# Constants and first row loads on POOL's queue, a longer filling product in short diagonals, image totals by transposes and a DVE sum

## The chip, the cores and the metric

The kernel runs on one core of a Trainium2 chip. The metric is the device time of one execution, in microseconds (us). A core has five engines, each with its own queue of instructions that it takes in order: PE (TensorE, matrix products and transposes into the PSUM memory), DVE (VectorE), ACT (ScalarE), POOL (GpSimd) and SP (SyncE, which here only issues DMA transfers). A DMA can be issued by SP, ACT or POOL; the data is then moved by sixteen DMA engines. PE's clock is granted by a throttle, and the profile shows the granted share of full speed (1.00, or 0.50 in stretches where it was halved). PSUM has eight banks, each of 128 partitions by 512 float32 elements.

## The reference

The input x has 16 images of 64 x 64 cells with 128 features. Three parts follow each other, each added to what it is given:

```python
x = x + lstm_2d(group_norm(x), ...)           # 32 groups of 4 features, statistics per image
t = x.reshape(16, 4096, 128)
t = t + attention(layer_norm(t), ...)         # 8 heads of 16, 64 landmarks
t = t + recurrent_ffn(layer_norm(t), ...)     # batch statistics, then yt = sigmoid(wx_t + yt @ V.T)
```

The two-dimensional LSTM computes a cell from its upper and its left neighbour: five gates, each a product of the normalised x by W and of the states by U, then `c = f0*c_u + f1*c_l + i*cp`, `h = o*tanh(c)`. The attention is the Nystrom form: with q and k averaged over 64 rows at a time into 64 landmarks per head,

```python
attn1 = softmax(q @ k_l.T); attn2 = softmax(q_l @ k_l.T); attn3 = softmax(q_l @ k.T)
out = attn1 @ pinv(attn2) @ (attn3 @ v) + conv33(v)      # pinv: six iterations
return (xn + (out @ w_out + b_out))
```

The softmax of `attn3` runs over all 4096 rows of an image, so its sums and `attn3 @ v` are gathered over the whole image before they can be used.

## The kernel before, in words

**Statistics of the images** (`group_stats`, 0 to 105 us). For each of the 16 images four loads of 512 KB, issued by SP (line 115), fill tiles `gs_xb` (twelve buffers). PE transposes each in blocks (line 118) into PSUM, DVE takes `bn_stats` of 512 columns (line 119), eight times an image, and one aggregate (line 120). Lines 121 and 122 call one function of the list `aside` behind an image, the first behind the fourth image (`b - 3`). The list is `jobs[:1] + loads + jobs[1:]`: `conv_bands` (eight small products that turn the convolution's weights into bands, and ACT's copy), four functions that load the rows of the first seven LSTM units (14 DMAs on ACT's queue), and `turn_weights` (a transpose of `ffn_w` and three ACT copies). Behind the images the late constants are loaded (SP), and PE, ACT, POOL and DVE make mean and inverse deviation (`centre`, `spread`), with products on the weights as filling between.

**Constants.** Ahead of it 17 DMAs on ACT's queue bring constants: four columns (`column`), three of `conv_lines` (`cb_line` from the weights, `cb_flat` in DRAM from `cb_line`, `cb_tm` from `cb_flat`, each waiting for the one before), and ten of `attention_tiles` (eight for `at_wo`, `at_bo`, `at_wf`). POOL fills tiles by memset and builds `head_mask` by two selections; DVE's `lm_side` (line 478) reads the mask, and stands in DVE's queue among the first statistics.

**LSTM** (`lstm_grid`, 105 to 1430 us). The cells of a diagonal are computed together, diagonal after diagonal, 190 slots; a diagonal has 16 columns of data per cell, from 16 up to 1024 and back, the middle ones cut into two halves. A slot issues the gates' products with U (line 288) on top of those with W that were begun earlier (line 283), the cell's arithmetic on DVE, POOL and ACT, and the later steps of the diagonals before. Where the diagonal is not cut and has at most 144 columns, `fill(384)` adds at the slot's end a product of 384 columns into the PSUM tile `ls_hq` whose result nobody reads (line 30 in `idle_products`).

**Attention** (1640 to 3470 us). After a first image's `first_step` and a mixed `second_step`, `step(s)` handles at once several groups of 512 rows in different stages: `new` (projections; largest scores of `attn3`, `greatest`, line 1028, and DVE's maxima, line 1032), `mid` (the group eight behind: `weigh`, exponentials line 1073, POOL's sum of weights line 1100, product with V), and `first`, `cur`, `third` to `sixth` (the groups some sixteen behind: `compare` line 1135, `topmost` line 1143, the softmax of `attn1`, output, normalisation, FFN input; `measure_feed` is DVE's statistics of the FFN input, line 1252). Eight groups make an image. Where an image starts (`q == 0`, 14 times in `step`) two more things are done: the image whose largest scores are complete gets its shifts (`shift` on POOL ends in `split`, lines 1040 to 1046; `turn_split` transposes it into bank 3, line 1011, ACT copies it), and the image whose weights are complete is gathered (`gather`): `im.sums`, the product of weights and values, is transposed into bank 2, and the sum over 512 weights per row, kept as four blocks of 128 partial sums `im.total`, is taken by four products by ones, line 1118 (eight instructions in the trace), also into bank 2; DVE takes the reciprocal (line 1121) and multiplies (`at_av`, line 1124); `spread_values` (line 1020) multiplies by the pseudo-inverse. `last_step` does the same at two starts, when only the late stages are left. `greatest` needs banks 0 to 3, `weigh` banks 4 and 5 and a pair of others, `turn_top` (line 1159) bank 2.

**Recurrence** (3470 to 3637 us): the FFN's scan, whose outputs POOL adds to the result by 64 DMAs (line 1600).

**Order.** In all these stages the instructions of an engine stand in the order of the program (`manual_schedule`); the constants and memsets ahead of them are placed by a planner that moves ready instructions ahead of waiting ones. A DMA issue is an instruction of its queue: while it waits for its source or for a semaphore, nothing behind it on that queue runs. The landing of a DMA is reported on a semaphore, which the program takes in turn from a fixed set.

Of the kernel before, what the change touches and what calls it, by code (L numbers as in the profile page):

```python
# [9 lines left out]
ALU = mybir.AluOpType  # L10
AX = mybir.AxisListType
# [3 lines left out]
P = 128  # L15
# [5 lines left out]
AHEAD = 7  # L21
# [34 lines left out]
def group_stats(nc, tc, x, ident, mhalf, gmean, grstd, aside, late, filler):  # L56
# [8 lines left out]
    with ExitStack() as ctx:  # L65
# [42 lines left out]
        for b in range(B):  # L108
            v = first if b < last.b0 else last
            rows = x[b].rearrange("i j f -> (i j) f").rearrange("(p k) f -> p k f", k=K)  # L110
            st = sp.tile([P, K // 4, 6], F32, tag="st", name="gs_st")
            for q in range(K // 4):
                if q % 2 == 0:
                    xb = ld.tile([P, 8, F], F32, tag="xb", name="gs_xb")
                    nc.sync.dma_start(out=xb, in_=rows[:, 4 * q : 4 * q + 8, :])
                tp = ps.tile([P, 4, P], F32, tag="tp", name="gs_tp")
                for k in range(4):
                    nc.tensor.transpose(tp[:, k, :], xb[:, q % 2 * 4 + k, :], ident)
                nc.vector.bn_stats(st[:, q, :], tp.rearrange("p k n -> p (k n)"))
            nc.vector.bn_aggr(v.mv[:, b - v.b0, :], st.rearrange("p q s -> p (q s)"))  # L120
            if 0 <= b - 3 < len(aside):
                aside[b - 3]()
            if b == last.b0:
                centre(first, nc.scalar.copy, nc.gpsimd)
# [53 lines left out]
def lstm_grid(nc, tc, x, fixed, stats, ident, mhalf, gmean, grstd, t1, acc, filler):  # L178
# [18 lines left out]
    with ExitStack() as ctx:  # L197
# [193 lines left out]
        def slot(t):  # L391
# [34 lines left out]
            if v and v.ns == S and v.cols <= NARROW:  # L426
                fill(384)

        with tc.manual_schedule(
# [4 lines left out]
        ):  # L434
            stats([lambda a=a: [load(v, nc.scalar) for v in units[a : min(a + 2, AHEAD)]] for a in range(0, AHEAD, 2)])
            wk = ctx.enter_context(tc.tile_pool(name="ls_wk", bufs=2, reuse_waits="tile"))
# [16 lines left out]
def column(nc, pool, vec, name):  # L453
    a = pool.tile([P, 1], F32, name=name)
    nc.scalar.dma_start(out=a, in_=vec.rearrange("(p o) -> p o", o=1))
    return a
# [283 lines left out]
def conv_lines(nc, pool, conv_w, dram):  # L740

    H, _, KS, _ = conv_w.shape
    T = 32
    W = T + KS - 1
    flat = dram.tile([H, T + W], F32, name="cb_flat")
    line = pool.tile([H, T + W], F32, name="cb_line")
    nc.vector.memset(line, 0.0)
    nc.scalar.dma_start(out=line[:, T - 1 : T - 1 + KS], in_=conv_w.rearrange("h a k c -> h (a k c)"))
    nc.scalar.dma_start(out=flat, in_=line)
    tm = pool.tile([T, H, W], F32, name="cb_tm")  # L750
    nc.scalar.dma_start(out=tm, in_=bass.AP(tensor=flat.tensor, offset=flat.offset, ap=[[1, T], [T + W, H], [1, W]]))
# [18 lines left out]
def attention_tiles(nc, cp, sp, ps, dram, late, shape, values, conv_w, w_out, b_out, ffn_w, ident):  # L770
# [6 lines left out]
    C = 4  # L777
# [6 lines left out]
    for h in range(H):  # L784
        r = PLACE[h] * W2 + h % 2 * DH
        nc.scalar.dma_start(out=wo[r : r + DH], in_=w_out[h * DH : (h + 1) * DH])
    B = values.shape[0]
# [6 lines left out]
    bo = cp.tile([P, F], F32, name="at_bo")  # L794
    nc.scalar.dma_start(out=bo, in_=b_out.rearrange("(o f) -> o f", o=1).to_broadcast([P, F]))
    wf = cp.tile([P, P], F32, name="at_wf")
    nc.scalar.dma_start(out=wf, in_=ffn_w)
    wfT = cp.tile([P, P], F32, name="at_wfT")
# [47 lines left out]
def attention(nc, tc, t1, gamma, beta, wqkv, ident, mhalf, fixed, xp, rows, qm, km, pinvT, vd, t2, wx, wx_stats, out, ahead):  # L846
# [20 lines left out]
    with ExitStack() as ctx:  # L867
# [140 lines left out]

        def turn_split(im):
            r = bank(3, [P, P])  # L1010
            nc.tensor.transpose(r, split.rearrange("p n s -> p (n s)"), ident)
# [101 lines left out]
        def gather(im):  # L1113

            at = bank(2, [P, C, P])
            nc.tensor.transpose(at[:, 0, :], im.sums, ident)
            for n in range(NP):
                nc.tensor.matmul(at[:, 1, W2 * n : W2 * n + 2], im.total[:, n, :], ones[:, 0:2], start=True, stop=True)
            im.AV = sm.tile([P, NP, DH], F32, tag="av", name="at_av")
            rs = sm.tile([P, NP], F32, tag="rs", name="at_rs")  # L1120
            nc.vector.reciprocal(rs, at[:, 1, :].rearrange("p (n c) -> p n c", n=NP)[:, :, 0])
            for j in range(2):
# [277 lines left out]
        def step(s):  # L1400
# [334 lines left out]
def kernel(ctx: ExitStack, tc: tile.TileContext, ins: dict, out: bass.AP):  # L1735
# [43 lines left out]
    with tc.tile_pool(name="at_c", bufs=1) as ac, tc.tile_pool(name="at_x", bufs=1) as xp, tc.tile_pool(  # L1779
# [4 lines left out]
        with tc.tile_pool(name="first", bufs=1) as first:  # L1784
# [5 lines left out]
            with tc.tile_pool(name="ls_c", bufs=1) as lc:  # L1790
# [46 lines left out]
```

## Time and profile before

| | us |
|---|---|
| three runs | 3631.91, 3635.04, 3635.63 |
| median | 3635.04 |
| the profiled execution's own time | 3638.43 |
| its span | 3636.9 |

The table of stretches, asked for by stage (busy us of each engine; granted clock, GB/s):

| stage | us | PE | DVE | ACT | POOL | clock | GB/s |
|---|---|---|---|---|---|---|---|
| statistics | 0 to 105 | 80.95 | 87.79 | 3.85 | 20.37 | 0.93 | 335 |
| LSTM | 105 to 1430 | 1296.63 | 1163.88 | 826.92 | 1031.65 | 0.99 | 78 |
| landmarks, pseudo-inverse | 1430 to 1640 | 195.08 | 104.40 | 91.13 | 69.64 | 1.00 | 32 |
| attention | 1640 to 3190 | 1535.03 | 1309.44 | 1236.38 | 1171.54 | 1.00 | 161 |
| last steps | 3190 to 3470 | 250.53 | 219.65 | 208.79 | 142.58 | 0.99 | 183 |
| recurrence | 3470 to 3637 | 141.68 | 97.61 | 132.78 | 53.47 | 0.95 | 223 |

How to read a profile's line: a group of instructions is given as line of the kernel, engine, operation, tile written <- tiles read, partitions x elements, count, then busy time and the mean duration of one in ns, then the idle time ahead of them and what ended it. In a timeline, the first number is the start in us from the span's start, the second the duration. In a list of waits, `SPq L115 <- DMA ls_xt<-in_x_dram: 3.9, 2, 2.8` says that SP's queue, at line 115, waited for the landing of that transfer 3.9 us in all, twice, at most 2.8. "PEld" is the load of weights into PE, which runs beside its products.

### The profile page before, as it was taken

The numbers are of one execution on the slowest core, as the hardware profiler recorded it, in microseconds if no ns is written. First come the engines' busy times: TensorE is split into PE (matmuls) and PEld (weight loads), VectorE is DVE, ScalarE is ACT, GpSimd is POOL, SyncE is SP. The second block draws the span as 40 slices with busy tenths as digits, with TensorE's granted clock in tenths as the row PEclk, the third lists the DMA queues.
The fourth block names the chain that finished last, engine by engine and source line by source line (L and its number), as shares of the span: only waits on it lengthen the run. The fifth ranks groups of instructions, "written<-read, shape, count | busy, mean of one in ns | idle before, by whom it ended". The sixth has DMA issues, their size and how long they took to land. (4 is left out here: it accounts for less than half of the span.)

```text
span 3636.9 us, 106193 instructions
## 1 busy us (share of the span) xinstructions
PE 3499.9 (96%) x40438; PEld 2343.7 (64%) x40438; DVE 2982.8 (82%) x7005; ACT 2499.9 (69%) x5126; POOL 2489.2 (68%) x3843
## 2 busy tenths in 40 slices
PE   7899999999999998999999999999999999997988
PEld 5666665545567666985666666666666666654777
DVE  8699999998889887544888888888888888888665
ACT  0466556656667665445788888888888888876787
POOL 1577877777788885434777777777777777785223
PEclk9999999999999999999999999999999999999999
DMA  9223232333333321023677777777777777667799
GB/s 339 83 76 80 80 86 80 84 84 83 85 88 86 81 76 38 4 63 92 147 185 187 164 162 163 166 167 163 164 166 166 165 164 168 157 143 187 201 273 182
DMA packets 834210, 484.50 MB, mean 133 GB/s; under 512 B 304672, under 2 KB 800672, under 8 KB 833696
## 3 DMA queue, kind: packets, MB, share of 16 engines
q1 hardware_dynamic: 814026, 442.55, 47.8%
q0 software_dynamic: 17728, 34.61, 5.3%
q8 instruction: 322, 5.28, 0.6%
q14 instruction: 192, 1.57, 0.1%
q10 hardware_dynamic: 1942, 0.50, 0.1%
HBM read 239.21 MB, written 238.29 MB: 131 GB/s over the span
## 5 line engine op out<-in xcount | busy, mean ns | idle before, releaser
L1100 POOL TENSOR_TENSOR at_total<-at_total,at_e 128x512 f32<-128x512 f32 x472 | 603.1, 1278 | 228.3 <-ACT at_e L1073 208.6
L290 ACT ACTIVATE ls_g<-ls_z,ls_b 128x304 f32<-128x304 f32 (+26 forms) x950 | 494.0, 545 | 225.0 <-PE ls_z L288 192.7
L283 PE MATMUL ls_z<-ls_xn,ls_w 128*128 128x432 f32 (+28 forms) x1700 | 586.1, 492 | 1.5 <-POOL ls_xn L275 1.2
L283 PEld LDWEIGHTS ls_z<-ls_xn,ls_w 128*128 128x128 f32 x1700 | 309.6, 191 | 189.4 <-issue 98.1
L288 PE MATMUL ls_z<-ls_hsum,ls_u 128*128 128x304 f32 (+26 forms) x1140 | 369.7, 461 | 0.0
L1032 DVE TENSOR_REDUCE at_mxq<-at_bank 128x1 f32<-128x512 f32 x512 | 314.9, 677 | 53.0 <-PE at_bank L1028 53.0
L323 POOL TENSOR_TENSOR ls_tt<-ls_ve,mhalf 128x8 f32<-128x8 f32 (+2 forms) x190 | 312.7, 1646 | 19.8 <-DVE ls_ve L322 4.2
L288 PEld LDWEIGHTS ls_z<-ls_hsum,ls_u 128*128 128x128 f32 x1140 | 211.6, 194 | 128.6 <-issue 78.4
L1177 ACT ACTIVATE at_eT<-at_bank 128x512 f32<-128x512 f32 x512 | 264.5, 604 | 42.1 <-PE at_bank L1172 41.5
L406 ACT ACTIVATE ls_g<-ls_cell 128x304 f32<-128x304 f32 (+26 forms) x190 | 93.2, 491 | 268.1 <-DVE ls_cell L405 267.8
L288 PE MATMUL ls_z<-ls_h,ls_u 128*128 128x304 f32 (+26 forms) x760 | 256.2, 460 | 12.3 <-DVE ls_h L410 12.3
L402 POOL TENSOR_TENSOR ls_g<-ls_g,ls_cell 128x304 f32<-128x304 f32 (+26 forms) x190 | 180.1, 948 | 127.7 <-ACT ls_g L290 113.0
L340 ACT ACTIVATE ls_tt<-ls_tt,ls_nb 128x128 f32<-128x128 f32 (+9 forms) x632 | 261.0, 478 | 5.6 <-POOL ls_tt L323 5.0
L979 PE MATMUL at_bank<-at_xT,wqkv 128*32 128x512 f32 (+1 forms) x1684 | 262.8, 602 | 2.0 <-DVE at_cmx L1143 1.1
L275 POOL TENSOR_TENSOR ls_xn<-ls_xn,grstd 128x272 f32<-128x272 f32 (+40 forms) x186 | 209.9, 1129 | 76.2 <-DVE ls_xn L270 71.2
L1143 DVE TENSOR_REDUCE at_cmx<-at_bank 128x8 f32<-128x512 f32 x256 | 175.6, 686 | 103.8 <-PE at_pair L1135 102.1
L1248 ACT COPY at_fx<-at_bank 128x512 f32<-128x512 f32 x128 | 133.7, 1044 | 142.9 <-PE at_bank L1244 138.3
L1619 DVE SCALAR_TENSOR_TENSOR rc_y<-rc_w,rc_scale,rc_z 128x256 f32<-128x256 f32 x344 | 154.6, 481 | 86.3 <-PE rc_z L1606 84.5
L1238 ACT ACTIVATE at_z<-at_u,at_nb,at_r 128x128 f32<-128x128 f32 x512 | 209.6, 484 | 4.6 <-POOL at_nb L1233 4.5
L288 PEld LDWEIGHTS ls_z<-ls_h,ls_u 128*128 128x128 f32 x760 | 141.9, 193 | 107.8 <-issue 53.2
L1600 POOL DMA_DIRECT2D out_dram<-rc_tt x64 | 77.4, 1209 | 168.4 <-ACT rc_tt L1597 145.0
L1193 DVE STREAM_TRANSPOSE at_t<-at_bank 128x512 f32<-128x512 f32 x256 | 167.9, 695 | 25.3 <-PE at_bank L1184 25.2
(281 smaller groups left out, 9683.8 us busy)
## 6 DMA issues: line engine op xcount, KB each, us to landing
at_win<-vd SPq DMA_DIRECT2D x256, 256.0 KB
t<-ls_tt SPq DMA_DIRECT2D x392, 130.0 KB
at_T<-t SPq DMA_DIRECT2D x128, 264.0 KB
gs_xb<-in_x_dram SPq DMA_DIRECT2D x64, 512.0 KB
at_xh<-t SPq DMA_DIRECT2D x128, 256.0 KB
vd<-at_v SPq DMA_DIRECT2D x128, 256.0 KB
t<-at_u SPq DMA_DIRECT2D x128, 256.0 KB
out_dram<-at_u SPq DMA_DIRECT2D x128, 256.0 KB
```

Of the source, the lines that this page charges most:

```text
L275: eng.tensor_tensor(a, a, norm(v, grstd), ALU.mult)
L283: nc.tensor.matmul(v.z[g][:, : v.total], wt[g], v.xn[:, : v.total], start=True, stop=True)
L288: nc.tensor.matmul(view(v, v.first.z[g]), ut[g], hin, start=False, stop=True, skip_group_check=True)
L290: nc.scalar.activation(a[:, : v.cols], z, AF.Tanh if g == 4 else AF.Sigmoid, bias=bt[g])
L323: nc.gpsimd.tensor_tensor(v.tt[:, 0:k, F + 2 : F + 4], ve[:, :, :k].rearrange("p r k -> p k r"), mhalf[:, : 2 * k].rearrange("p (k r) -> p ...
L340: nc.scalar.activation(v.tt[:q, k, F + 4 :], v.tt[:q, k, 0:F], AF.Identity, bias=v.nb[:q, k : k + 1], scale=v.tt[:q, k, F + 3 : F + 4],)
L402: nc.gpsimd.tensor_mul(v.a[1], v.a[1], v.cl)
L979: nc.tensor.matmul(out[r], lhsT[:, r], rhs, start=True, stop=True)
L1032: nc.vector.tensor_reduce(gr.im.mxq[:, n : n + 1, gr.g], gr.s[n], AX.X, ALU.max)
L1100: eng.tensor_tensor(total, total, e[:, :, c, :], ALU.add)
L1177: nc.scalar.activation(gr.eT[:, n], gr.s[n], AF.Exp)
L1238: nc.scalar.activation(gr.z[:, c, :], gr.u[:, c, :], AF.Identity, bias=gr.nb[:, c : c + 1], scale=gr.r3[:, c : c + 1])
```

## The change

Three edits.

1. The 17 constants and the 14 row loads of the first LSTM units are issued by POOL's queue (`nc.gpsimd`) instead of ACT's. In `group_stats` the list `aside` starts behind the seventh image instead of the fourth, and it holds the loads first, then `conv_bands` and `turn_weights`.
2. In diagonals of at most 64 columns (`4 * B`) the filling product of 384 columns is followed by one of 256.
3. `gather` transposes the four blocks of `im.total` into bank 2, DVE sums the 512 columns and takes the reciprocal; the transpose of `im.sums` goes to bank 3. In `step`, `gather` comes earlier, right behind `topmost`, at the place where `measure_feed` stands in the other steps (which then comes behind `measure(fourth, (2, 3))`), and `turn_split` uses bank 2 instead of 3.

```diff
-            if 0 <= b - 3 < len(aside):
-                aside[b - 3]()
+            if 0 <= b - 6 < len(aside):
+                aside[b - 6]()
...
-                fill(384)
+                fill(384, *[256] * (v.cols <= 4 * B))
...
-            stats([lambda a=a: [load(v, nc.scalar) for v in units[a : min(a + 2, AHEAD)]] for a in range(0, AHEAD, 2)])
+            stats([lambda a=a: [load(v, nc.gpsimd) for v in units[a : min(a + 2, AHEAD)]] for a in range(0, AHEAD, 2)])
...
-    nc.scalar.dma_start(out=a, in_=vec.rearrange("(p o) -> p o", o=1))
+    nc.gpsimd.dma_start(out=a, in_=vec.rearrange("(p o) -> p o", o=1))
...
-        nc.scalar.dma_start(out=wo[r : r + DH], in_=w_out[h * DH : (h + 1) * DH])
+        nc.gpsimd.dma_start(out=wo[r : r + DH], in_=w_out[h * DH : (h + 1) * DH])
...
-        def turn_split(im):
-            r = bank(3, [P, P])
+        def turn_split(im, k=3):
+            r = bank(k, [P, P])
...
-            at = bank(2, [P, C, P])
+            total, at = bank(2, [P, NP, P]), bank(3, [P, 1, P])
+            for n in range(NP):
+                nc.tensor.transpose(total[:, n, :], im.total[:, n, :], ident)
             nc.tensor.transpose(at[:, 0, :], im.sums, ident)
-            for n in range(NP):
-                nc.tensor.matmul(at[:, 1, W2 * n : W2 * n + 2], im.total[:, n, :], ones[:, 0:2], start=True, stop=True)
...
-            nc.vector.reciprocal(rs, at[:, 1, :].rearrange("p (n c) -> p n c", n=NP)[:, :, 0])
+            nc.vector.tensor_reduce(rs, total, AX.X, ALU.add)
+            nc.vector.reciprocal(rs, rs)
...
-            if sixth:
+            if start and was:
+                gather(was.im)
+            elif sixth:
                 measure_feed(sixth)
...
-            if start and was:
-                gather(was.im)
...
-                turn_split(mid.im)
+                turn_split(mid.im, 2 if was else 3)
...
+            if start and was and sixth:
+                measure_feed(sixth)
...
-                        group_stats(nc, tc, x, ident, mhalf, gmean, grstd, jobs[:1] + loads + jobs[1:], late, wqkv)
+                        group_stats(nc, tc, x, ident, mhalf, gmean, grstd, loads + jobs, late, wqkv)
```

The other constants (`cb_line`, `cb_flat`, `cb_tm`, `at_bo`, `at_wf`) are edited in the same way as `at_wo`.

More of the change, by code (lines that the diff above doesn't have):

```diff
@@ L747, in conv_lines @@
     nc.vector.memset(line, 0.0)
-    nc.scalar.dma_start(out=line[:, T - 1 : T - 1 + KS], in_=conv_w.rearrange("h a k c -> h (a k c)"))
-    nc.scalar.dma_start(out=flat, in_=line)
+    nc.gpsimd.dma_start(out=line[:, T - 1 : T - 1 + KS], in_=conv_w.rearrange("h a k c -> h (a k c)"))
+    nc.gpsimd.dma_start(out=flat, in_=line)
     tm = pool.tile([T, H, W], F32, name="cb_tm")
-    nc.scalar.dma_start(out=tm, in_=bass.AP(tensor=flat.tensor, offset=flat.offset, ap=[[1, T], [T + W, H], [1, W]]))
+    nc.gpsimd.dma_start(out=tm, in_=bass.AP(tensor=flat.tensor, offset=flat.offset, ap=[[1, T], [T + W, H], [1, W]]))
     turn = pool.tile([T, T], F32, name="cb_turn")
@@ L794, in attention_tiles @@
     bo = cp.tile([P, F], F32, name="at_bo")
-    nc.scalar.dma_start(out=bo, in_=b_out.rearrange("(o f) -> o f", o=1).to_broadcast([P, F]))
+    nc.gpsimd.dma_start(out=bo, in_=b_out.rearrange("(o f) -> o f", o=1).to_broadcast([P, F]))
     wf = cp.tile([P, P], F32, name="at_wf")
-    nc.scalar.dma_start(out=wf, in_=ffn_w)
+    nc.gpsimd.dma_start(out=wf, in_=ffn_w)
     wfT = cp.tile([P, P], F32, name="at_wfT")
```

## The prediction

> **What bounds the kernel now.** I read the page of the profile first. PE is busy 96% of the span, but a share over stages with different limits says little, so I went by stretches: the first 105 us (statistics of the sixteen images), the diagonals up to 1430 us, and the attention steps from 1640 to 3190 us.
>
> ```profile
> PE 3499.9 (96%) x40438; PEld 2343.7 (64%) x40438; DVE 2982.8 (82%) x7005; ACT 2499.9 (69%) x5126; POOL 2489.2 (68%) x3843
> ```
>
> Second, the table by stretches of 10 us (stretch, length, busy PE, PEld, DVE, ACT, POOL, granted clock, DMA share, GB/s).
>
> ```profile
> 10.00:20.00 10.00, 4.89 (x30) 4.03 (x28) 4.82 (x10) 1.28 (x1) 8.61 (x15) 0.92 0.76 260
> 20.00:30.00 10.00, 8.59 (x61) 7.09 (x60) 9.51 (x18) 0.00 (x0) 7.98 (x19) 0.91 1.01 398
> 40.00:50.00 10.00, 5.65 (x32) 4.50 (x32) 6.18 (x11) 0.00 (x0) 0.00 (x0) 0.78 0.79 233
> 50.00:60.00 10.00, 6.95 (x46) 6.45 (x47) 6.39 (x11) 0.00 (x0) 0.00 (x0) 0.71 0.98 370
> 80.00:90.00 10.00, 9.17 (x64) 6.43 (x62) 9.93 (x19) 0.00 (x0) 0.00 (x0) 1.00 1.02 419
> ```
>
> Undisturbed, DMA brings 419 GB/s and DVE is full (9.93 of 10). From 10 to 20 and from 40 to 60 us both drop. Third, the waits of SP's queue say why:
>
> ```profile
> SPq L115 <- DMA ls_xt<-in_x_dram: 3.9, 2, 2.8
> SPq L115 <- DMA cb_tm<-cb_flat: 3.8, 1, 3.8
> SPq L115 <- DMA cb_flat<-cb_line: 2.6, 1, 2.6
> SPq L115 <- DMA at_wo<-in_L_attn_w_out_dram: 1.2, 2, 0.8
> ```
>
> A load of x (line 115) has no use for these constants and rows, and yet waits for them. The trace gives each issue the semaphore of its landing: SP's and ACT's issues take turns on the same eight (100, 102 to 108), so a new issue waits for the landing eight issues back, whoever issued it; POOL's 68 issues use eight others (111 to 118). While ACT issues 17 constants (1.0 to 13.4 us) and 14 row loads (34.1 to 44.8 us), few of the eight places hold a 512 KB load of x.
>
> Fourth, the timeline of one step that starts an image (line 1135 at 1932.72 us):
>
> ```profile
> 1936.53 0.95 PE L1118 MATMUL at_bank<-at_ones,at_total 128*128 128x2 f32 x8
> ...
> 1937.18 0.22 POOL L1046 TENSOR_SCALAR at_split<-at_mx 128x4 f32<-128x4 f32 x1
> ...
> 1937.46 0.33 PE L1011 MATMUL at_bank<-ident,at_split 128*128 128x128 f32 x1
> ...
> 1937.74 0.46 DVE L1124 TENSOR_TENSOR at_av<-at_bank,at_rs 64x64 f32<-64x64 f32 x2
> ...
> 1938.85 0.62 PE L1028 MATMUL at_bank<-at_KT,qm 32*128 32x512 f32 x2
> ...
> 1942.72 0.38 PE L1159 MATMUL at_bank<-at_identb,at_top 128*128 128x128 bf16 x4 [0.47 <-ACT at_g L1022]
> ```
>
> An ordinary step takes 12.69 us (1920.04 to 1932.72) with PE without a gap; this one 15.80. Fifth, the filling product in a short diagonal, while the clock is 0.5 and late at full clock:
>
> ```profile
> 116.72 1.65 PE L30 MATMUL ls_hq<-wqkv,ident 128*128 128x384 f32 x2
> ```
>
> ```profile
> 1414.61 0.91 PE L30 MATMUL ls_hq<-wqkv,ident 128*128 128x384 f32 x2 [0.88 <-DVE ls_tt L301]
> ```
>
> **The sum's base.** The profiled execution took 3638.43 us (span 3636.9); the median of the runs shown is 3635.04, 3.4 us lower. I add up against 3638.43 and take 3.4 off at the end.
>
> **Part 1: constants and first row loads on POOL.** DVE paces the statistics: in the undisturbed images the aggregates (line 120) are 5.14 us apart (68.49, 73.63, 78.76). Sixteen make 82.2 us. The first statistic starts at 6.80 and the last aggregate ends at 104.82, so 15.8 us are stalls: the gaps between aggregates exceed 5.14 by 3.1 and 4.2 us in the first two images (constants) and by 2.9 and 5.5 us in the sixth and seventh (row loads). With POOL issuing, all eight places hold loads of x, 10 us of transfer at 1.25 us each.
>
> What stays: the first six statistics run 0.85 us apart at the cold clock instead of 0.64, 1.4 us in all; DVE's wait of 1.4 us for `lm_side`, which needs POOL's second selection of `head_mask` at 13.02; and what small packets take from x, for which no row exists: 0.48 MB at 419 GB/s is 1.2 us, and I take 1.5. POOL itself: its 31 new issues have no row here. The bounds are ACT's own issues (0.30 to 0.77 us) and POOL's output DMAs (64 at 1.209 us, line 1600); I take 1.209, the same engine: 37 us of a queue that idles 70.0 us before line 95, so later work is covered. Early it is not: POOL stands 8.65 us before its first selection, `cb_flat` waits for `cb_line` (2.93 to 7.88 us before) and `cb_tm` for `cb_flat` (7.94 to 12.04), now with POOL's queue behind them. If two or three issues slip in front of the second selection, `lm_side` comes 2.5 to 3.5 us later. I take 2.9. Sum: 15.8 - 1.4 - 1.4 - 1.5 - 2.9 = 8.6 us gained, bounds 13.0 (no slip, no loss to packets) and a loss (rival 1). Late issues, `load` of SP and the centring chain keep their places behind the last aggregate. Moving `conv_bands` and `turn_weights` behind the 11th and 12th image (before: the fourth and ninth) shifts 0.91 and 0.27 us of PE that DVE's pace hides; without that cover they would cost just these.
>
> The Trainium skill says otherwise. "DMA: Bandwidth & Descriptors", section "Issuing engines are not separate DMA queues", holds that DMAs from scalar, sync and gpsimd end on the same 16 engines and that spreading them saves only issue time. By the waits above, what is shared here is the eight places and not the engines, whose share falls to 0.76. By that page of the Trainium skill this part would bring 0; this trace shows the waits and cannot show the rest.
>
> **Part 2: filling products.** A 256-wide product is added where a diagonal has at most 64 columns: four at the beginning, four at the end. The 384-wide one holds PE for 0.75 us at full clock (1414.61 until the next gate product at 1415.36), so 256 cost 0.50, cold 1.0. The first diagonal hides it in a gap of 0.39 us; in the others the fill stands on the chain, since it waits for `ls_tt` and the next gates queue behind it: 0.1 + 7 x 0.50 = 3.6 us. Gain: the clock was 0.5 from 113.9 to 127.6 us. Gate to gate the diagonals there took 4.51 and 4.58 us, at full clock a like one 3.07 (1412.29 to 1415.36): 2.9 us; the third is cold for 4.8 us, at the same ratio 1.5; at the end (cold 1417.8 to 1428.0) 0.46 and 0.8. Sum 5.7, net 2.1 gained if the clock holds. For the clock I count what share of a stretch of 3.4 us the moving columns fill, at 0.35 us per 416 of them (the gate products at 128 us, full clock): it fell after 0.29, 0.38, 0.41 and 0.42, and held after 0.45, 0.46 and more, and once after 0.41 (at 38.8 us). With 256 more, the first diagonals come to an estimated 0.47 to 0.54, the last one to 0.42. So I take 2.0; bounds 4 gained (half of the fills hidden), 4 lost (the clock falls anyway).
>
> The Trainium skill's "TensorE: Matmul & The Clock Gate", section "HAM oscillation", puts the rule as no idle gaps over some 3.4 us. PE had no gap over 1.1 us before the fall at 113.9, so by that rule a fill changes nothing and costs 3.6.
>
> **Part 3: image totals, banks apart.** Fourteen starts lie in `step`. Removed: eight products by ones (0.95 us) and DVE's reciprocal from bank 2; added: four transposes (line 960: four in 0.61 us) and a sum over 512 elements (like line 1032, 0.68 us). PE's saving of 0.3 us is worth nothing: `turn_split` waits for POOL's `split`, ready at 1937.40, before and after. What counts is behind it. `greatest` and `weigh` take 2.25 us in an ordinary step and 2.86 here, because bank 2 is held until `at_av` ends at 1938.20 and bank 3 until ACT has copied the split at 1938.10. After: topmost ends at 1936.31, sum 0.69, reciprocal 0.18, `at_av` 0.46: bank 3 free at 1937.75. `measure_feed` (0.68 us) leaves this place and fits into DVE's idle 1.2 us before line 1193. Bank 2, now with the split, is free at about 1938.2, as the queries' copy comes 0.7 us later; the third product is due then. So 0.5 of the 0.61 goes: 14 x 0.5 = 7.0. In `last_step` the first start gains some 0.5 (1.7 us of cold products by ones), the second loses 0.2 and the sum stands on DVE's path there (0.7, partly covered). I take 6.5; bounds 0 (ACT's exponentials set line 1159 anyway) and 14 x 0.8 = 11.
>
> Sum: 8.6 + 2.0 + 6.5 = 17.1; 3638.4 - 17.1 = 3621.3, less 3.4: **3618 us**.
>
> **Rivals.** (1) POOL's queue bounds the start, the slower side. If `head_mask`'s second selection falls behind all 17 constants, it comes at 2.2 + 8.65 + 17 x 1.209 + 5.0 (`cb_line`'s landing) + 4.1 (`cb_flat`'s) = 40.5 us; DVE, at `lm_side` by 12, stands 29 us instead of 1.4. The sum moves with that wait one for one: 4.3 us of it are in, 21 level the change, 29 make 3643. For it: between the two selections (10.86 and 13.02 us) five other ready instructions ran, and a waiting issue blocks POOL; against: the selection needs none of the constants. (2) Small packets slow the 16 engines whoever issues them, so x comes as late as before: parts 2 and 3 alone, 3626.5. For it: from 10 to 20 and 40 to 50 us, with constants and rows under way, 260 and 233 GB/s arrived; against: the engines' share was 0.76 and 0.79 then, with SP waiting. By the page of the Trainium skill quoted above the time would come out so. (3) The clock falls anyway: part 2 costs 4 instead of 2 gained, 3624. (4) Banks give nothing since ACT's copy of `at_g` sets line 1159: 3624.5.
>
> **Chances.** Forecast 0.46 (own range 3610 to 3623), rival 3 0.13, rival 4 0.12, rival 2 0.14, rival 1 0.15, of which 0.12 above 3642. A measurement tells about 0.2%, 7.3 us (3627.8 and 3642.3). Faster: 0.46 + 0.13 + 0.12 and 0.05 of rival 2 (what part 1 then still brings) = 0.76; slower 0.12; same 0.09 + 0.03 = 0.12. The range leaves out rival 1's upper part and, below, what part 1's and part 3's upper bounds give together: 3606 to 3634.
>
> **What would show it.** Part 1: the last aggregate near 96 us, SP's waits for constants gone, 419 GB/s from 6 us on; wrong if DVE's wait for POOL at `lm_side` exceeds 10 us. Part 2: no clock of 0.5 around the first diagonals. Part 3: steps that start an image at 15.3 us, line 1028 without its gap. The forecast fails if POOL holds DVE, or if x is still slowed while POOL's DMAs are under way.

## The result, and the profile after

The changed kernel takes 3624.25 us (median of seven runs, 3618.05 to 3626.08); the kernel before takes 3636.01 us (median of seven, 3631.91 to 3640.54). The ratio is 0.9964 with a 95% interval of 0.9952 to 0.9975: 11.8 us by the medians, against 17.1 forecast. The time lies inside the range of the prediction and on the side that it gave. The profiled execution took 3622.92 us, 1.3 below its median, with a span of 3621.3 us; that of before was 2.4 above its median, so the two profiles are 15.5 us apart.

The page's line of busy times, of the changed kernel:

```profile
PE 3485.2 (96%) x40390; PEld 2327.3 (64%) x40390; DVE 2991.0 (83%) x7021; ACT 2498.0 (69%) x5126; POOL 2509.7 (69%) x3874
```

PE has 48 instructions fewer (four at each of 16 gathers, less 16 of the fills), DVE 16 more (the sums), POOL 31 more (the DMA issues). None of the shares shows where the time went. In the statistics, the table by stretches does (stretch, length, busy PE, PEld, DVE, ACT, POOL, granted clock, DMA share, GB/s):

```profile
10.00:20.00 10.00, 7.96 (x46) 6.44 (x45) 5.63 (x11) 0.00 (x0) 5.79 (x14) 1.00 1.01 403
20.00:30.00 10.00, 9.40 (x64) 6.48 (x62) 9.93 (x19) 0.00 (x0) 6.95 (x11) 1.00 0.98 393
40.00:50.00 10.00, 9.39 (x64) 6.43 (x62) 9.93 (x19) 0.00 (x0) 9.47 (x21) 1.00 1.03 418
50.00:60.00 10.00, 7.81 (x57) 5.93 (x56) 9.93 (x18) 0.00 (x0) 1.82 (x4) 1.00 1.03 358
80.00:90.00 10.00, 8.87 (x66) 6.98 (x66) 9.93 (x19) 0.17 (x1) 0.64 (x3) 1.00 1.02 405
```

From 20 us on DVE is full (9.93 of 10). The last aggregate ends at 94.58 us instead of 104.82. (Single profiles differ here: in two kernels of the experiments below whose start is that of the kernel before, it ends at 103.56 and 106.93.) The trace gives SP's issues eight landing semaphores and POOL's 99 issues eight others, and the waits of SP's queue up to 110 us hold no constants and no rows any more:

```profile
SPq L115 <- DMA gs_xb<-in_x_dram: 54.2, 55, 2.9
SPq L126 <- DMA gs_xb<-in_x_dram: 7.1, 8, 0.9
SPq L115 <- PE gs_tp L118: 2.4, 8, 0.7
SPq L348 <- DVE ls_tt L301: 1.4, 1, 1.4
```

What is left of the stalls is in DVE's waits of the first 20 us: PE's first transposes, and POOL's mask.

```profile
DVE gs_st L119 <- PE gs_tp L118: 3.7, 5, 2.1
DVE lm_side L478 <- POOL head_mask L465: 3.6, 1, 3.6
```

Now the attention. A step that starts an image is called a start below. In the timeline of one (line 1136 at 1921.96 us) the new operations stand where the prediction put them, but the products of line 1028 are still torn apart, seven records and one:

```profile
1924.81 0.66 PE L1117 MATMUL at_bank<-ident,at_total 128*128 128x128 f32 x4
1925.50 0.69 DVE L1121 TENSOR_REDUCE at_rs<-at_bank 128x4 f32<-128x512 f32 x1
1926.70 0.33 PE L1011 MATMUL at_bank<-ident,at_split 128*128 128x128 f32 x1 [0.27 <-POOL at_split L1046]
1926.96 1.55 PE L1028 MATMUL at_bank<-at_KT,qm 32*128 32x512 f32 x7
1927.07 0.27 ACT L1013 CAST at_minus<-at_bank 128x128 bf16<-128x128 f32 x1
1927.99 0.59 PE L1028 MATMUL at_bank<-at_KT,qm 32*128 32x512 f32 x1
```

The step takes 15.66 us instead of 15.80.

The filling products in the short diagonals at the start run at full clock, 384 and 256 columns in four records of 1.34 us together:

```profile
108.84 1.34 PE L30 MATMUL ls_hq<-wqkv,ident 128*128 128x384 f32 x4 [0.53 <-DVE ls_tt L301]
```

Set side by side, with a stage measured from one instruction to another, the two profiles differ as follows (us; the stages are read off the timelines):

| from | to | before | after | difference |
|---|---|---|---|---|
| start | last aggregate | 104.82 | 94.58 | -10.2 |
| first product of the states (line 288) | the same, five slots later | 22.83 | 18.42 | -4.4 |
| then | last gate product | 1287.33 | 1287.53 | +0.2 |
| last gate product | first product of `greatest` (line 1028) | 201.45 | 205.04 | +3.6 |
| first product of line 1172 (1173 after) | the same in the first of the last steps | 1465.41 | 1463.63 | -1.8 |
| then | eight steps on | 91.66 | 90.51 | -1.2 |
| then | end | 356.75 | 354.88 | -1.9 |

Stages left out differ by less than 0.15 us. The fourth row is a stage that no edit touches, and the last holds only one `gather`, at the second start of the last steps; both rows are taken up below.

### The profile page after: what moved, and what is told of

Read it like the earlier page. It is cut to its first block, busy times and chain, and to the rows that moved or that the text cites. A ratio compares the mean times of both kernels' runs of the same rounds, so it can differ in the third digit from the quotient of the medians.

```text
span 3621.3 us, 106150 instructions
## 1 busy us (share of the span) xinstructions
PE 3485.2 (96%) x40390; PEld 2327.3 (64%) x40390; DVE 2991.0 (83%) x7021; ACT 2498.0 (69%) x5126; POOL 2509.7 (69%) x3874
## 5 line engine op out<-in xcount | busy, mean ns | idle before, releaser
L1609 PE MATMUL rc_z<-rc_y,rc_vT 128*128 128x256 f32 x688 | 171.3, 389 | 12.8 <-ACT rc_y L1630 12.1
```

## The experiments

### Each edit alone, and the split in another bank

Four kernels were run in one group, with 27 runs of the kernel before (median 3633.76). The median of before differs between groups by up to 4 us, so a kernel is compared with the runs of before of its own group. The first has only the edits of the queue:

```diff
-    nc.scalar.dma_start(...)                  # 17 constants
+    nc.gpsimd.dma_start(...)
-            stats([... load(v, nc.scalar) ...])
+            stats([... load(v, nc.gpsimd) ...])
-            if 0 <= b - 3 < len(aside):       # and jobs[:1] + loads + jobs[1:]
+            if 0 <= b - 6 < len(aside):       # and loads + jobs
```

> The first edit alone (17 constants and 14 row loads on POOL's queue, `aside` behind the seventh image, loads first). Theory: the loads of x no longer wait for landings of constants and rows, because POOL's issues have landing semaphores of their own; the last aggregate ends near 94.6 us instead of 104.8, and the time is some 10 us below before (about 3626). Rival: small packets slow x whoever issues them, and the 10 us seen at the last aggregate of the changed kernel come from elsewhere; then less than 3 us. The stretch from the last gate product of the LSTM to the first product of the attention, 201.4 us before and 205.0 in the changed kernel, should stay at 201 to 202 here if the filling products are what lengthened it.

Measured: 3626.58 us, ratio 0.9982 (0.9973 to 0.9991), 7.2 us by the medians. The last aggregate ends at 95.86 us, and the aggregates are 5.13 us apart from the second to the last. SP's waits are those of the changed kernel, but for one line:

```profile
SPq L115 <- PE gs_tp L118: 12.2, 27, 1.2
```

SP now waits for free buffers: the loads run ahead of PE and DVE. The rival falls as an account of the whole, since the same small packets are under way. The stretch from the last gate product to the attention took 200.1 us.

The second kernel has only the filling product:

```diff
-                fill(384)
+                fill(384, *[256] * (v.cols <= 4 * B))
```

> The second edit alone (256 columns more in diagonals of at most 64 columns). Theory: the clock stays at 1.00 through the first diagonals, which gains some 4.4 us up to the eleventh slot (22.8 us from the first gate product before, 18.4 in the changed kernel); at the end the four products cost 0.43 us each and the clock falls later, net about 0. Then some 4 us faster, 3632, unless the stretch up to the attention is longer by 3 us again, which would leave 1 us (3635). Rival: the gain at the start in the changed kernel was due to the statistics ending without stalls, not to the filling products; then the clock falls here as before, near 114 us, and the time is 1 to 3 us above before.

Measured: 3629.01 us, ratio 0.9989 (0.9980 to 0.9998), 4.8 us. From the first product of the states to the same five slots later (the expectation calls this the eleventh slot, as each product of the trace has two records) it took 18.63 us, at a clock of 1.00:

```profile
109.60:128.30 18.70, 16.85 (x97) 12.44 (x96) 10.37 (x52) 8.73 (x34) 8.39 (x23) 1.00 0.06 18
```

So it was the fills, and not the statistics without stalls. The eleven runs lie between 3627.01 and 3632.13, those of before between 3627.89 and 3639.52: the lower end is the same, the upper one is cut. The other profiles, one of each kernel, suggest why. With 384 columns alone, the clock fell in the first diagonals of four profiles and held in two. In all of them it changes only on a fixed grid: the four changes in the kernel before at 113.92, 127.57, 1417.81 and 1428.05 us are 4, 382 and 385 times 3.413 us apart from the first. One step of this grid is called a stretch here, and its filled share is counted as in the prediction:

| kernel, 384 columns alone | five slots, us | clock 0.5 | filled share of the first stretches of 3.4 us |
|---|---|---|---|
| before | 22.83 | 113.9 to 127.6 | 0.29 |
| the third edit alone | 22.78 | 115.7 to 129.4 | 0.35 |
| order alone (below) | 22.86 | 114.5 to 128.2 | 0.37 |
| the first edit alone | 21.32 | 106.6 to 116.9 | 0.57, 0.45 |
| constants alone (below) | 16.93 | none | 0.53, 0.45, 0.46 |
| rows alone (below) | 16.94 | none | 0.53, 0.45, 0.45 |

Line by line the diagonals are the same in all six. What differs is where the edges of the 3.4 us stretches fall: 0.4 to 0.7 us ahead of the first product of the states in the first two rows, 1.6 to 1.7 in the last two, where the products before it share a stretch with the thin first diagonal. In the third an edge comes 0.6 behind it; in the fourth it is 2.1 ahead, and the clock fell one stretch later, after a share of 0.45 that held elsewhere, so the count has no sharp bound. The table by stretches shows both cases (columns as above; first the kernel before, then the one with the row loads moved alone):

```profile
110.90:133.70 22.80, 21.33 (x87) 15.27 (x87) 10.67 (x52) 9.63 (x34) 8.42 (x23) 0.70 0.05 13
```

```profile
106.30:123.20 16.90, 15.04 (x87) 10.85 (x87) 10.38 (x52) 8.72 (x34) 8.34 (x23) 1.00 0.07 21
```

So 256 columns more cost 18.42 - 16.93 = 1.5 us in these four diagonals where the clock would have held, and save 22.83 - 18.42 = 4.4 where it would have fallen. In the last ten slots it is 33.1 us (384, clock held), 34.6 to 34.8 (384, clock fell) and 34.4 (with 256): 1.3 paid, 0.2 to 0.4 saved. That the place of the stretch decides is read from six profiles and a count; no run set it on purpose. The spread of the times fits it: a fall of 13.65 us at half clock lowers the mean clock of a run by 0.0019, and among the 27 runs of before the two with a mean of 0.988 took 3637.9 us on average, the ten with 0.990 took 3633.7, the one with 0.992 took 3627.9.

The third kernel has only the edit of `gather` and of the split's bank (its diff is the last part of the change's).

> The third edit alone (four transposes and a DVE sum, `gather` earlier, split in bank 2). By the changed kernel's trace: the fourteen starts take 15.66 instead of 15.80 us, 1.9 us in all; the first start of the last steps 17.6 instead of 19.0. So 3 us faster, 3633. Had the prediction's 0.5 us a start been right and something else in the changed kernel hidden it, it would be 7 to 8 us (3628).

Measured: 3632.27 us, ratio 0.9994 (0.9985 to 1.0003): 1.5 us, not clear of none. The starts take 15.66 us here too, so nothing else in the changed kernel hid the 0.5 us; it was never there. The way through all attention steps (fifth row of the table above), which no fall of the clock in the LSTM reaches, takes 1464.6 to 1466.1 us in the six kernels without this edit and 1462.7 to 1463.8 in the three profiles with it: 2.1 us between the means.

The fourth kernel is the changed one, with

```diff
-                turn_split(mid.im, 2 if was else 3)
+                turn_split(mid.im, 4 if was else 3)
```

> The changed kernel with the split transposed into bank 4 instead of bank 2. Theory: the four products of `greatest` run side by side in four row groups and are all due when the first starts, so any bank among 0 to 3 that waits for ACT's copy of the split holds half of them for 0.4 to 0.6 us; in bank 4 nothing waits: the starts take 15.25 instead of 15.66 us, 14 x 0.41 = 5.7 us below the changed kernel (3618.5). Rival: ACT's exponentials and its copy of `at_g` set the next product (line 1160 in the changed kernel) anyway; then the starts stay within 0.1 us and the time at 3624.

Measured: 3617.85 us, ratio to before 0.9956 (0.9943 to 0.9970). The starts take 15.38 us, 0.28 less instead of 0.41, and the way through the attention steps 1459.7 us, 3.7 less than with bank 2. In the timeline of a second run of this kernel the products of line 1028 stand together, and output (line 1213) follows 2.29 us behind their start, against 2.79 before, 2.66 with bank 2 and 2.18 in an ordinary step (the prediction's 2.86 and 2.25 start 0.07 us earlier). Behind it, line 1160 waits for ACT's copy of `at_g`:

```profile
1925.67 0.33 PE L1011 MATMUL at_bank<-ident,at_split 128*128 128x128 f32 x1 [0.27 <-POOL at_split L1046]
1925.93 1.25 PE L1028 MATMUL at_bank<-at_KT,qm 32*128 32x512 f32 x8
1928.22 1.16 PE L1213 MATMUL at_bank<-at_wo,at_oT 128*128 128x128 f32 x8
1930.51 0.38 PE L1160 MATMUL at_bank<-at_identb,at_top 128*128 128x128 bf16 x4 [0.56 <-ACT at_g L1022]
```

The theory holds for the bank: it was the bank of the split that tore the products apart. The rival holds in part. At each of the fourteen starts this line waits for `at_g`, in the kernel before (0.47 us in the line that the prediction shows), with bank 2 (0.47) and with bank 4 (0.56). But ACT's exponentials, which stand ahead of that copy, themselves follow `greatest` and `weigh`: they begin 7.78, 7.64 and 7.35 us behind the step's first `compare`. So they come earlier when the products do. Of the 0.37 us that PE gains on the way to output, 0.09 is lost again in the longer wait for ACT; this leaves the 0.28.

That second run, in the last group (before there 3637.92):

> The changed kernel with the split in bank 4 once more, on the same chip as the two built on it: 16 us below the kernel before, the starts at 15.38 us.

Measured: 3620.91 us, ratio 0.9955 (0.9942 to 0.9969), 17.0 us below before; starts 15.37.

### What of the queue's edit counts

Two kernels share the first edit between them. One moves the 17 constants only:

> Only the 17 constants on POOL's queue; the row loads stay on ACT's queue, behind the fifth to eighth image, and `conv_bands` behind the fourth, as before. Theory (shared landing places): the stalls of the first two images go, those of the sixth and seventh stay (8.4 us in the gaps between their aggregates); the last aggregate near 102 to 103 us, as POOL's later mask takes some 2 us back of the 7.3: 2 to 3 us faster. A new risk: `conv_bands` behind the fourth image now waits for `cb_tm`, which POOL issues near 28 us, and PE's transposes stand behind it: some 5 us between 33 and 38 us. Rival (packets): the first two images stay as slow as before.

Measured: 3636.76 us, ratio 0.9998 (0.9988 to 1.0007). The first images run without stall from the first aggregate on (18.77, 23.91, 29.05, 34.18), but the fifth to eighth take 9.0, 5.1, 9.9 and 8.3 us, and the last aggregate ends at 107.84, 3 us later than in the profile of before. SP's waits say what holds the loads, and PE's what came new, `conv_bands` on constants that POOL now brings late:

```profile
SPq L115 <- DMA ls_xt<-in_x_dram: 15.4, 6, 9.5
```

```profile
PEld gs_tp L118 <- issue: 8.3, 3, 5.2
POOL cb_tm L751 <- DMA cb_flat<-cb_line: 3.1, 1, 3.1
PEld cb_t L766 <- POOL at_pairs L817: 2.1, 1, 2.1
PE cb_t L766 <- DMA cb_tm<-cb_flat: 1.9, 1, 1.9
```

The other moves the 14 row loads and the order only:

> Only the 14 row loads on POOL's queue, with the list behind the seventh image and the loads first; the 17 constants stay on ACT's queue. Theory: the stalls of the sixth and seventh image go (8.4 us), those of the first two stay (7.3 us, with 1.4 us of them behind `lm_side`); the last aggregate near 96.5 us, 8 us faster than before (3626), nearly all that the first edit brings, since what the constants' move gains it loses again at `lm_side`. Rival: both moves share the 9 to 10 us evenly.

Measured: 3633.50 us beside 3637.61, ratio 0.9990 (0.9981 to 0.9999): 4.1 us, half of what was expected. The last aggregate ends at 100.21 instead of 96.5. The sixth image still loses 3.1 us and the fifth 0.4: POOL, free of constants, issues the rows between 28 and 38 us, SP waits for no row, but x is late. Neither my theory's 8 us nor an even share is right: at the last aggregate of single profiles the two halves alone gain 4.6 and lose 3.0 us, together they gain 9.0 to 10.2. It seems that the constants have to be away for x to have a lead when the rows come.

The third leaves all on ACT and changes only the order:

```diff
-            if 0 <= b - 3 < len(aside):
-                aside[b - 3]()
+            if 0 <= b - 6 < len(aside):
+                aside[b - 6]()
...
-        group_stats(..., jobs[:1] + loads + jobs[1:], late, wqkv)
+        group_stats(..., loads + jobs, late, wqkv)
```

> The kernel before with only the order of the list changed: the row loads behind the seventh to tenth image, `conv_bands` and `turn_weights` behind the 11th and 12th, all DMAs still on ACT's queue. Since ACT's row loads wait for nothing once nothing stands before them in its queue, they are issued as soon as the constants are, before 25 us. Theory (shared landing places): the stalls of 8.4 us move from the sixth and seventh image to the ones where the rows are now issued, but are not removed: last aggregate 101 to 105 us, within 3 us of before. Rival: it was the place in the order and not the queue that helped; then the last aggregate comes near 96.

Measured: 3636.67 us beside 3637.92, ratio 1.0001 (0.9992 to 1.0010). ACT issues the rows from 22.07 to 32.30 us, the second to sixth aggregate come 10.0, 6.2, 9.5, 5.6 and 6.6 us after the one before, the rest 5.1, and the last ends at 104.44. SP's waits name the rows again:

```profile
SPq L115 <- DMA gs_xb<-in_x_dram: 48.5, 44, 4.2
SPq L115 <- DMA ls_xt<-in_x_dram: 12.4, 8, 3.1
```

The stalls moved with the issues and were not removed. On ACT's queue the order alone is worth nothing; the queue, and with it the set of landing semaphores, is. With the constants on POOL the later place of `conv_bands` counts too, as the first of these three kernels shows. That it is the semaphores and not something else that comes with the queue rests on the waits: no run gave ACT's issues a set of their own.

### DVE's wait for the mask

```diff
 def head_mask(nc, pool, ident, heads):
-    nc.gpsimd.memset(mask, 1.0)
-    ...                                       # two selections on POOL
+    nc.vector.tensor_reduce(mask, ident.rearrange("p (h d) -> p h d", h=heads), AX.X, ALU.add)
```

> The kernel with the split in bank 4, and the head mask summed by DVE from the identity in place of POOL's memset and two selections. Theory: DVE's `lm_side` stood 3.6 us in the changed kernel behind POOL, which needed 11.5 us before its first selection; without it the statistics run on: the first aggregate near 13 us instead of 17 to 19, the last near 91.5 instead of 94.6 to 95.9, 3 to 3.5 us below the kernel with the split in bank 4. Rival: the loads of x come too late for the second image anyway (DVE waited for PE and PE for x in the first 11 us), so the wait moves from POOL to x and less than 1 us is gained.

Measured: 3620.96 us, ratio 0.9956 (0.9942 to 0.9969), no better than without this edit (0.9955 and 0.9956). The first aggregate did come at 13.74 us, and the last at 95.13. Between 28 and 62 us DVE waits as it does not in the changed kernel, for PE, and PE for x:

```profile
DVE gs_st L119 <- PE gs_tp L118: 3.1, 5, 1.3
PE gs_tp L118 <- DMA gs_xb<-in_x_dram: 8.0, 17, 1.6
```

The rival's end, at another place than it said: a new wait, for x, of the size of the one taken away. The rates show why. In the changed kernel, too, x slows while POOL's DMAs are under way (table by stretches, second column from the right the share of the DMA engines, last GB/s):

```profile
40.00:46.00 6.00, 5.70 (x40) 3.92 (x38) 5.97 (x12) 0.00 (x0) 5.93 (x15) 1.00 1.03 420
50.00:56.00 6.00, 4.66 (x34) 3.43 (x34) 5.96 (x11) 0.00 (x0) 1.82 (x4) 1.00 1.05 341
```

The engines are fully busy in both, but with rows under way they bring 341 GB/s instead of 420: 1.86 MB for x and 0.17 MB, in 256 packets, on POOL's queue. (The packets of the rows run from 46 to 57 us; the first issue is at 43.45.) The prediction had named this as a sign that it would fail. There DVE does not notice, because its 3.6 us at `lm_side` had given x a lead. So the page of the Trainium skill that the prediction quoted ("DMA: Bandwidth & Descriptors", section "Issuing engines are not separate DMA queues") is right on the engines: the transfers of SP and of POOL do share them, as 420 against 341 shows. What it says of the gain, that another issuer saves only issue time, the measurement contradicts: 7.2 us with the first edit alone.

### Rows behind the statistics

On top of the mask on DVE the row loads are emitted behind the 15th image's `centre`:

```diff
             if b == last.b0:
                 centre(first, nc.scalar.copy, nc.gpsimd)
+                for load in loads:            # the 14 row loads, on POOL's queue
+                    load()
```

> The kernel with the mask on DVE and the split in bank 4, and the 14 row loads emitted behind the 15th image's `centre`, so that POOL issues them near 85 us instead of 42 to 50; `conv_bands` and `turn_weights` stay behind the 11th and 12th image. Theory: with the mask on DVE the statistics gained 3.5 us at the first image and lost them again at the fifth to ninth, because x came at 293 to 330 GB/s while small packets of POOL's DMAs were under way (32 to 36 and 48 to 56 us) and its lead was gone; without the rows there the stalls of the eighth and ninth image go (1.6 us), those of the fifth and sixth, beside `at_wo`, `at_bo` and `at_wf`, stay: last aggregate near 93.5 instead of 95.1. Rival: x is late there for another reason (its own queue), then 95 as before. Risk: the rows land only when the LSTM's first unit waits for them; from the last aggregate to the first gate product then more than 6.06 us.

Measured: 3616.60 us, ratio 0.9949 (0.9935 to 0.9962). The aggregates are 5.14 us apart from the first to the last, which ends at 92.09 us: the rows were the cause of the late x, of more of it than was expected. But the first product of the states starts at 100.55 us, as in the changed kernel (100.64): the last aggregate is 2.5 us earlier and the way from it 2.4 longer. POOL's timeline and DVE's waits show who holds it:

```profile
89.45 4.55 POOL L256 DMA_DIRECT2D ls_xt<-in_x_dram  x8
94.08 0.28 POOL L104 TENSOR_SCALAR gs_ve<-gs_ve 128x14 f32<-128x14 f32 x1
94.45 2.64 POOL L105 TENSOR_TENSOR grstd<-gs_ve,mhalf 128x14 f32<-128x14 f32 x1
```

```profile
DVE ls_xn L277 <- POOL grstd L105: 2.7, 1, 2.7
```

The 14 issues (7.91 us from 86.10) stand ahead of the power that makes `grstd`, and DVE waits for that: the wait for the mask, which became a wait for x, is now a wait for POOL. The 4.3 us between this kernel and the split in bank 4 in the same group (3616.60 against 3620.91) therefore don't come from the start. In the profiles it is another stage: from the last gate product to the attention the second has 204.7 us and the first 200.0, and this stage varies by itself, as the next section shows.

The last kernel is this one with the filling product only at the beginning (`v.cols <= 4 * B and v.d < D0`):

> As the one before, but with the 256 columns more only in the four short diagonals at the beginning, not in the last four. Theory: the last ones cost 0.3 us each where the clock holds (33.1 to 33.2 us for the last ten slots with 384 columns at full clock, 34.4 with 640) and save 1.5 us where it falls; 0 to 1.3 us faster than the one before, and more spread between executions.

Measured: 3616.37 us, ratio 0.9943 (0.9929 to 0.9956): no difference to the one before that these runs can tell, with a wider spread (3613.84 to 3622.65 against 3615.95 to 3620.82). Its profiled execution is the slowest of the five. The last ten slots took 33.1 us, as expected. But the clock fell at 100.1 us, ahead of all the longer fills: the stretch before holds PE's wait behind `grstd` (2.1 us) and none of them, and was filled to 0.31 (five slots took 24.84 us). The kernel before this one, with the same instructions there, kept its clock: there the stretches begin 0.6 us later against the products, and are filled to 0.41 and 0.43.

```profile
92.40:101.40 9.00, 6.65 (x34) 4.40 (x33) 1.96 (x15) 0.00 (x0) 5.77 (x8) 0.93 0.29 74
101.40:126.20 24.80, 23.72 (x96) 17.67 (x96) 10.61 (x52) 9.50 (x34) 8.42 (x23) 0.68 0.03 7
```

### The changed kernel again

> The changed kernel once more, unedited, for a second profile and times on the same chip as the others. In the first profile of it the stretch from the last gate product to the attention took 205.0 us, in the five other kernels 199.8 to 201.5. If this was that execution alone, it is 200 to 202 here; if it belongs to the changed kernel, 205 again. The time beside the kernel before: 10 to 14 us less.

Measured: 3626.09 us beside 3637.61, ratio 0.9968 (0.9956 to 0.9980). The stretch from the last gate product to the attention took 208.1 us. So it isn't the one execution. Nothing shows that it is the edit either: the kernel with the split in bank 4 has the same instructions up to there and took 201.2 and 204.7, the others 199.8 to 203.2. What differs in the waits is time in which PE waited for nothing that the profile shows, here the changed kernel's second run and then the first run with bank 4:

```profile
PE lm_bank L585 <- issue: 10.0, 16, 2.4
```

```profile
PE lm_bank L585 <- issue: 6.3, 8, 2.1
```

Eight more such stops make 3.7 of the 6.9 us; the rest I have not accounted for, and what the stops are, no run here tells.

## Why the prediction was right or wrong

**The whole.** 17.1 us were forecast, 11.8 came. The three edits alone bring 7.2, 4.8 and 1.5 us in one group, 13.5 in sum, with intervals of 3 us to each side, so that no disturbance of one by another is shown. That the whole came near is in part luck: part 3 lacks 5.0 us and part 1 lacks 1.4, and part 2 brought 2.8 too many. Rivals 3 and 4 named 3624 and 3624.5, the measured time itself; the total can't tell them from the forecast, only the single edits can.

**Part 1: right, in mechanism and nearly in size.** 8.6 us forecast, 10.2 at the last aggregate of the profile, 7.2 by medians. Within the sum, several terms were off, and their errors partly cancel. POOL's issue was priced at 1.209 us from the output DMAs; the 14 row loads took 7.91 us, 0.57 each, so that the nearest row of the same engine was twice too dear, and ACT's 0.30 to 0.77 was the better one. The slip of two or three issues ahead of the second selection was one (`attn_beta`, 0.74), but `attn_gamma` went ahead of the first, and POOL then stood 11.50 us instead of 8.65: the mask came at 15.0 us instead of 13.2, 1.8 later, where 2.9 had been taken. The cold transposes, 1.4 us, stayed: up to 13.70 us PE's first transposes start 0.21 us apart, twice the 0.11 of warm ones, and the first statistics 0.85 as before (the clock's record begins only at 14.28, with 1.00). But DVE, held by the mask until 15.04, would have been no earlier without them, so the two terms should not have been added. "What small packets take from x", 1.5 us by bytes, was too small as a loss of transfer: 341 against 420 GB/s over 6 us alone is 1.1 us, and the kernel that took x's lead away lost 3.1 us to it. In the changed kernel it is hidden, by the very wait for the mask that was counted as a loss.

**Rivals 1, 2 and 3.** The selection did not fall behind the constants: the wait stayed at 3.6 us, and only 21 would have used up the gain. Rival 2 is refuted as an account of the whole by the first edit alone (7.2 us where it gave none), but its mechanism exists and sets the floor once the mask is out of the way. Rival 3 is refuted by the clock: it held in the first diagonals in seven of the eight profiles that have the longer fills there, and in the eighth it had fallen ahead of them.

**Part 2: right in mechanism, smaller in cost and larger in gain.** 2.0 us forecast, 4.2 in the profiles, 4.8 by medians. The eight fills cost 1.5 + 1.3 = 2.8 us where 3.6 were counted. The fall of the clock at the start costs 5.9 us (22.83 against 16.93) and the one at the end 1.5, 7.4 together, where 5.7 were counted. What the step lacked is that the fall is not a property of the kernel alone: with 384 columns it came in four of six profiles. Its bounds by filled share were too sharp as well: the clock fell after 0.45 with the first edit alone, and held after 0.41 and 0.43 with the rows behind the statistics. The rule of the Trainium skill weighed there ("TensorE: Matmul & The Clock Gate", section "HAM oscillation": no idle gaps over some 3.4 us) would have made the fill a cost of 3.6; the medians give a gain of 4.8 (interval 0.7 to 7.3), so the count of moving columns was the better guide.

**Part 3: wrong.** 6.5 us forecast, 1.5 by medians (interval up to none), 3.0 in the profiles: 1.8 from the fourteen starts and 1.2 from the last steps. The step that failed is: "Bank 2, now with the split, is free at about 1938.2, as the queries' copy comes 0.7 us later; the third product is due then. So 0.5 of the 0.61 goes". The four products of `greatest` do not follow each other; they run side by side in four groups of rows (in an ordinary step all start within 0.02 us), so the third was due with the first, at 1937.72. The sentence itself says that bank 2 comes free at the time at which it had come free before. The split only moved the wait from one bank to another, and 0.13 us a start went. In bank 4, outside the set, the whole 0.50 us goes between these products and output (2.79 to 2.29). Rival 4 has the price nearly right. Its mechanism is half right: line 1159 does wait for ACT's copy of `at_g` at every start, before and after. But that copy itself moves with the products ahead of it, by 0.28 us a start with the split in bank 4, so banks do count.

**Last steps and recurrence.** The first start of the last steps was to gain 0.5; it took 17.6 instead of 19.0 in the profiles, and 17.4 to 19.8 in all the profiles with the edit, 18.1 to 20.6 in those without (means 18.0 and 19.1), with falls of the clock between 3169 and 3200 us in each. The second start was to lose 0.2; it takes 10.50 us with the edit and 10.33 without, in every profile. The last row of the table (-1.9) is within what that stretch shows among the kernels without the edit (354.7 to 358.1) and among those with it (354.9 to 358.2), so it is no gain.

## What to carry to other kernels

A load that waits for "somebody else's" landing is a sign that issuers share a set of landing semaphores; moving the other issues to a queue with its own set frees it, but the bytes still share the engines (341 instead of 420 GB/s here), and only a lead in the loads hides that.

Before a buffer is moved between banks, ask when the product that needs it is due: the four products in different groups of rows were all due at once here, and a bank outside of their set cost 0.11 us against an ordinary step instead of 0.48.

Where a wait is removed in a chain in which two resources run at nearly the same pace (DVE 82.2 us, x 80 us: 64 loads of 0.524 MB at 419 GB/s), name the next one first: here three waits in a row (3.6, 3.1 and 2.7 us) had nearly the same price.

## What the runs showed of the hardware that I had not expected

Kernels with the same diagonals kept or lost the clock in them, which made 6 us; by six profiles it goes with where the 3.4 us stretches happened to start. With the longer fills alone the runs spread over 5 us instead of 12. POOL's DMA issues took 0.48 to 0.75 us for loads against 1.209 for the outputs that add. POOL's stop ahead of its first selection was 8.65 us before and 11.50 after one DMA issue. In the pseudo-inverse PE stops 8 to 16 times for 0.6 to 0.9 us each on average without any wait that the profile shows, and the number differs between executions of the same instructions.
